# A transformer layer on one core: a batch's list of side work turned by eight groups, so that half of the left pieces and four Q and K pieces stand in the batch before

## The chip, the cores and the metric

The kernel runs on one core of a Trainium2 chip. The metric is device time in microseconds. Three runs of the kernel before gave 2230.23, 2231.86 and 2234.39 us: a median of 2231.86 us.

## The reference

The input is x of 8 batches, 1024 rows and 256 columns, in float32. The layer is an attention block with a residual and a layer norm, and a feed-forward block with the same around it.

```
Q, K, V = x Wq^T + bq, x Wk^T + bk, x Wv^T + bv        16 heads of 16 columns
scores  = Q K^T / 4 + lambda * mask                    mask[i, j]: two bells in |i - j|
x1      = layernorm(x + softmax(scores) V Wo^T + bo)
h       = x1 ternary(w_fc)^T + gate * (x1 v^T fast_b^T u^T)
out     = layernorm(x1 + max(h, 0)^2 ternary(w_proj)^T)
```

`ternary(w)` rounds each row of a weight matrix to -1, 0 or 1 times the mean size of the row. The hidden width is 1024.

## The kernel before, in words

**Groups.** The attention is worked through in groups. A batch has four sets of four heads; each set has two halves of 512 queries (a *step* is one set and one half); a step has 8 blocks of 128 keys. One group treats one block of keys for the four heads, so a step has 8 groups, a batch 64 and the kernel 512. We call a group's place in its batch +0 to +63.

In each group TensorE does, in this order: the scores `e` of the group (L714, four matmuls; where the block lies near the half's diagonal, four more from `prior` at L724 add the mask); the *pieces* of side work of this group; the scores `s` of the group twelve places later (L647, four matmuls), from which VectorE finds each query's maximum (L659); and the weighted sum `av` of the group before (L753, eight matmuls). ScalarE takes exponentials of `e` (L738). Scores share three PSUM buffers in turn. Each block of eight groups turns its finished maxima with a matmul (L675) at places +5, +13, +21 and so on; they go through DRAM (`rows`) into the stacks from which the scores are made (L691). Every sixteen groups `fill_stack` loads the stacks of a coming set, eight DMAs of 256 KB, at +0, +16, +32 and +48.

**Pieces.** All other work is cut into pieces for two small PSUM halves (`misc`), and each piece has a matmul part and an `empty` part that follows on ScalarE, GpSimd or VectorE:

- `transpose_x` (L540): turns a quarter of a half of x of the coming batch into `xT`; eight pieces. The two halves of x share one buffer, and the fourth piece asks for the second half.
- `queries_keys(b, c)` (L593): Q and K of eight heads, eight pieces, K and Q by turns for the first half of the rows and then for the second. Every second piece casts a full half into `two` (ScalarE, L612), subtracts on GpSimd (L613) and writes the result to DRAM (`parts_k`, `parts_q`). `two` has one buffer.
- `values` (L566): V, eight pieces.
- A *chunk* of 256 rows of the feed-forward: two projections P (L953), two turns T (L987), one low rank L (L1000), eight hidden H (L1027) and four output O (L1062). A batch has four chunks. `first_chunk` makes the first chunk's row load and the addition of its bias ride on other pieces.

Projections need the heads divided by their sums: `normalize` hangs steps on later groups. For the second half of the heads, these are a load of the sums at +1 of the next batch, an inversion at +3, loads at +4, and divisions of the two halves on GpSimd at +6 and +8 (L810).

Each P, Q/K and V piece has a cost number of 0.86, O 0.93, H 0.6, L 0.48, T 0.23 and `transpose_x` 0.22. A group has room for two halves of `misc`. While the rest of the list would fit into the rest of the batch at one piece a group, a group stops at a fill of over 0.75; otherwise it goes on.

**The list of a batch.** `jobs_of(b)` (L1372 to L1411) writes the batch's pieces in order. For batches 1 to 6 the list before is: the load of x; eight pieces of Q and K of the second half of the heads of this batch (`qk`), with the eight pieces left over from the list before (`over`) and the first four transposes of x of batch b + 1 among them; four V pieces; and the feed-forward of batch b - 1, with four transposes, the eight Q/K pieces of the first heads and four V pieces of batch b + 1 among it. The last eight pieces of it (four H, four O) are left over. Batch 0 has no feed-forward yet and prepares the ternary weights instead (L442, L475, L519), in which a chain of small VectorE instructions (L460 to L466) follows each row block. Batch 7 has no batch to prepare for. After group 511 the last batch's feed-forward runs alone.

Every engine executes its instructions in the order in which they are written; the waits are derived from the tiles.

Of the kernel before, what the change touches and what calls it, by code (L numbers as in the profile page):

```python
# [30 lines left out]
WIDE = LEFT + 8 * P  # L31

LEAD = 12

KEPT = 8


@with_exitstack
def tile_postln_layer(
# [21 lines left out]
    B, L, D = x.shape  # L61
    NH = D // HD
    NG = NH // HG
    NB = L // P
# [32 lines left out]
    def load_x(b, half, tag="x"):  # L97
        t = p1.tile([P, QB, D], F32, tag=tag, name=f"x_{b}_{half}")
        nc.sync.dma_start(t, x[b, ts(half, HALF), :].rearrange("(t p) d -> p t d", p=P))
        x_of[b, half] = t  # L100
# [261 lines left out]
    now, jobs = -LEAD, []  # L362
# [966 lines left out]
    def with_(f, piece):  # L1329
        return (piece[0], lambda: (f(), piece[1]())[1], *piece[2:])  # L1330
# [33 lines left out]
    over = []  # L1364

    def first_x(b, main):

        for f, n in zip(first_chunk[b][0], (-8, -2)):
            main[n] = with_(f, main[n])
        return main  # L1370

    def jobs_of(b):  # L1372


        qk = queries_keys(b, 1, misc)
        load, early_xv, ahead = [], [], []
        if b + 1 < B:
            load = [(0.0, lambda: load_x(b + 1, 0), 0)]
            xs, vs = transpose_x(b + 1, misc), values(b + 1, misc)
            early_xv, ahead = xs[:4] + vs[: NB // 2], xs[4:]  # L1380
            ahead = ahead + queries_keys(b + 1, 0, misc) + vs[NB // 2 :]
        if b + 1 < B:
            first_chunk[b] = chunk(b, 0, misc)
        if b == 0:
            main = [(0.3, prepare_v, 1)] + [u for i in range(2) for u in prepare_fc(i)]
            main += [u for i in range(D // P) for u in prepare_proj(i)]
            side = ahead[:12] + early_xv[4:] + ahead[12:]
            return load + qk + early_xv[:4], first_x(b, spread(main, side, 0.05, 0.9))
        old = [over[k : k + 2] for k in range(0, len(over), 2)] or [[]] * 4
        if ahead:  # L1390
            t, q, v = ahead[:4], ahead[4:12], early_xv[4:] + ahead[12:]

            lead = [t[0], t[1], q[0], t[2], q[1], t[3], q[2], q[3], v[4], q[4], q[5]]
            at_end = [[q[6], q[7]], [v[5], v[6]], [v[7]], []]
            main = v[:4] + feed_forward(b - 1, misc, lead, at_end)
            t = early_xv[:4]
        else:

            old_o = old[2] + old[3]
            t, old[2:], lead = [()] * 4, [[], []], [qk[6], qk[7], *old_o]  # L1400
            main, qk = feed_forward(b - 1, misc, lead), qk[:6]
            load = [(0.0, f, 0) for k in (2, 3) for f in (ends[k]["load"], ends[k]["bias"])]
            for f, n in zip((ends[0]["load"], ends[0]["bias"]), (-8, -2)):
                main[n] = with_(f, main[n])
        t = [list(u for u in (k,) if u) for k in t]
        jobs = load + [qk[0], *old[0], qk[1], *old[1], *qk[2:4]]

        jobs += [*old[2], *t[0], qk[4], *t[1], *old[3], *t[2], qk[5], *t[3], *qk[6:]]
        over[:] = main[-KEPT:] if b + 1 < B else []
        main = main[:-KEPT] if b + 1 < B else main  # L1410
        return jobs, first_x(b, main) if b + 1 < B else main  # L1411

    def ready(u):
# [47 lines left out]
        *e0["H"][4:],  # L1463
    ]
    rest, es = None, {}
    jobs = [u for part in jobs_of(0) for u in part]

    v_first, qk_first, jobs[:7] = values(0, misc), jobs[1:7], jobs[:1]
    early = [u for two in zip(v_first, qk_first) for u in two] + v_first[6:]
    for g in range(-LEAD, total + 1):  # L1470
# [5 lines left out]
        if 0 <= g < total and g % per_batch == 0:  # L1476
            if g:
                assert not jobs
                jobs = [u for part in jobs_of(g // per_batch) for u in part]
        if g == total - 7:  # L1480

            old, jobs = jobs, []
# [157 lines left out]
```

## Time and profile before

| What | us |
|---|---|
| median of three runs | 2231.86 |
| the profiled execution | 2231.73 |
| its span | 2229.9 |
| TensorE busy in the span | 2160.5 |
| VectorE busy | 1591.5 |
| ScalarE busy | 1442.7 |
| GpSimd busy | 902.7 |
| before group 0 | 59.7 |
| batch 0 | 254.2 |
| batch 1 | 265.8 |
| a middle batch | 263.7 |
| batch 7 | 260.7 |
| after the start of group 511 | 70.7 |

The rows of batches are times from the first `e` matmul of one batch to that of the next, by the timeline. The profile is one execution on the chip. PE is TensorE's matmul, PEld its weight load, DVE VectorE, ACT ScalarE, POOL GpSimd, SP the engine that issues most DMAs. A line of the timeline has the start in us, the length in us, the engine, the source line, the instruction, what it writes and reads, the shapes, a count, and in brackets the idle time of the engine before it and what ended that.

### The profile page before, as it was taken

To read this page: it belongs to the slowest core of one execution; us is meant where nothing else is said; L and a number is where in the kernel's file an instruction comes from. 1 tells how busy PE (TensorE), PEld (TensorE's weight loads), DVE (VectorE), ACT (ScalarE), POOL (GpSimd) and SP (SyncE) were. 2 spreads that over 40 slices of the span, in tenths; PEclk is the share of its full clock that TensorE was granted. 3 is DMA by queue.
4 is the path that set the end of the run, shared out by engine and by line. 5 is a ranking of instruction groups with operands and counts; after the bars stand their busy time and mean duration, and the time that the engine had idled before them with its cause. 6 is when DMAs were issued, how large, how long until landed. Compare 5 with 4: busy or idle time off the path is not lost.

```text
span 2229.9 us, 36851 instructions
## 1 busy us (share of the span) xinstructions
PE 2160.5 (97%) x13144; PEld 1258.9 (56%) x13144; DVE 1591.5 (71%) x2952; ACT 1442.7 (65%) x2155; POOL 902.7 (40%) x1024
## 2 busy tenths in 40 slices
PE   6999999999999999999999999999999999999997
PEld 3444445555555555556555555555655555555557
DVE  6777776777777776777777777677777777677736
ACT  2665566666666667666666667676666666666654
POOL 4133322445333453245533444335443345444444
PEclk8999999999999999999999999999999999999998
DMA  7433334123433224423333223421344321422010
GB/s 194 109 92 89 74 96 114 66 71 75 118 115 87 56 56 119 129 71 80 75 125 103 73 67 92 130 87 52 75 118 116 87 71 46 132 70 53 22 46 20
DMA packets 110572, 193.36 MB, mean 87 GB/s; under 512 B 21100, under 2 KB 50108, under 8 KB 110388
## 3 DMA queue, kind: packets, MB, share of 16 engines
q1 hardware_dynamic: 108972, 189.42, 30.8%
q8 instruction: 104, 1.70, 0.3%
q10 hardware_dynamic: 1416, 1.58, 0.2%
q14 instruction: 80, 0.66, 0.1%
HBM read 105.19 MB, written 85.69 MB: 86 GB/s over the span
## 4 chain that ended last, share of the span: by engine, by line
PE 82%; DVE 8%; POOL 1%; issue 1%; ACT 1%; DMA 1%; SPq 0%; POOLq 0%; DVEq 0%; ACTq 0%
PE e L714 22%; PE av L753 19%; PE s L647 15%; DVE junk L659 6%; PE e L724 5%; PE misc L1027 4%; PE misc L593 4%; PE misc L1062 4%; PE misc L953 2%; PE misc L566 2%; PE misc L1034 1%; ACT exp L738 1%; DVE st L911 1%; PE misc L987 1%; PE misc L540 0%
## 5 line engine op out<-in xcount | busy, mean ns | idle before, releaser
L659 DVE CUSTOM_DVE_ANT_0 junk<-s,wide 128x1024 f32<-128x1024 f32 x1024 | 1248.6, 1219 | 534.3 <-PE s L647 492.0
L738 ACT ACTIVATE exp<-e 128x1024 f32<-128x1024 f32 x1024 | 1027.6, 1025 | 622.4 <-PE e L724 376.3
L714 PE MATMUL e<-st_q,st_k 66*128 66x512 f32 (+1 forms) x2048 | 664.6, 425 | 0.6 <-ACT exp L738 0.3
L714 PEld LDWEIGHTS e<-st_q,st_k 66*128 66x128 f32 (+1 forms) x2048 | 324.1, 189 | 463.3 <-ACT exp L738 82.5
L753 PE MATMUL av<-exp,v 128*17 128x512 f32 x4096 | 540.8, 600 | 0.0
L647 PE MATMUL s<-st_k,st_q 64*128 64x512 f32 x2048 | 400.5, 447 | 43.7 <-DVE pm L659 26.7
L647 PEld LDWEIGHTS s<-st_k,st_q 64*128 64x128 f32 x2048 | 167.3, 185 | 179.5 <-DVE pm L659 66.7
L737 DVE TENSOR_TENSOR e<-e,wide 128x372 f32<-128x372 f32 (+2 forms) x376 | 190.8, 507 | 47.0 <-PE e L714 41.9
L1045 POOL TENSOR_TENSOR rl<-rl 128x512 f32<-128x512 f32 x112 | 116.6, 1041 | 250.8 <-ACT hi L1044 243.4
L724 PEld LDWEIGHTS e<-prior,ident_r 128*128 128x128 f32 x1056 | 159.7, 190 | 24.2
L753 PEld LDWEIGHTS av<-exp,v 128*17 128x17 f32 x4096 | 68.1, 95 | 185.6 <-issue 184.5
L724 PE MATMUL e<-prior,ident_r 128*128 128x244 f32 (+2 forms) x1056 | 157.7, 272 | 0.0
L1047 POOL TENSOR_TENSOR lo<-rl,hi 128x512 fp32r<-128x512 f32 x112 | 143.9, 1285 | 8.8
L576 POOL TENSOR_TENSOR v<-v,bv_row 128x256 f32<-128x256 f32 x64 | 43.8, 686 | 213.4 <-ACT v L575 213.4
L1082 POOL TENSOR_TENSOR r<-r,sp_row 128x256 f32<-128x256 f32 x56 | 41.2, 735 | 205.1 <-ACT r L1081 205.1
L1027 PE MATMUL misc<-xhi,wfT 128*128 128x256 f32 x448 | 116.0, 282 | 0.2 <-ACT fullq L608 0.2
L1027 PE MATMUL misc<-xlo,wfT 128*128 128x256 f32 x448 | 115.1, 280 | 0.0
L1062 PE MATMUL misc<-wpT,lo 128*128 128x256 f32 x448 | 111.7, 283 | 2.1 <-POOL lo L1047 2.1
L1062 PE MATMUL misc<-wpT,hi 128*128 128x256 f32 x448 | 113.8, 287 | 0.0
L613 POOL TENSOR_TENSOR twok<-fullk,twok 128x512 fp32r<-128x512 f32 x30 | 38.6, 1288 | 163.0 <-ACT twok L612 163.0
L1040 ACT ACTIVATE rl<-misc,s_fc 128x256 f32<-128x256 f32 x224 | 94.3, 475 | 0.2
L1062 PEld LDWEIGHTS misc<-wpT,lo 128*128 128x128 f32 x448 | 85.1, 190 | 6.3 <-POOL lo L1047 2.9
(241 smaller groups left out, 2353.8 us busy)
## 6 DMA issues: line engine op xcount, KB each, us to landing
st_k<-parts_k SPq DMA_DIRECT2D x128, 256.0 KB
st_q<-parts_q SPq DMA_DIRECT2D x124, 256.0 KB
parts_k<-twok SPq DMA_DIRECT2D x60, 512.0 KB
parts_q<-twoq SPq DMA_DIRECT2D x64, 256.0 KB
parts_q<-twoq SPq DMA_DIRECT2D x30, 512.0 KB
x<-in_L_attn_x_dram SPq DMA_DIRECT2D x16, 512.0 KB
raw_o<-avs SPq DMA_DIRECT2D x248, 32.0 KB
rec<-back SPq DMA_DIRECT2D x30, 256.0 KB
```

What stands on the lines that cost most here:

```text
L647: nc.tensor.matmul(pair[a][:, kh, :], stack["q", s, pr, a][rows, ts(blk, P)], stack["k", s, pr, a][rows, ts(kh, HALF)], start=True, stop=True,
L659: nc.vector.tensor_tensor_reduce(out=junk, in0=t.rearrange("p k n -> p (k n)"), in1=wide[:, LEFT - P * blk : LEFT - P * blk + L], scale=1. ...
L714: nc.tensor.matmul(t[:, a, :], stack["k", s, pr, a][rows, ts(blk, P)], stack["q", s, pr, a][rows, ts(h, HALF)], start=True, stop=not by_pe,)
L724: nc.tensor.matmul(t[:, a, lo - HALF * h : hi - HALF * h], ident_r, prior[:, n, lo - first : hi - first], start=False, stop=(n == 1),)
L737: nc.vector.tensor_add(part, part, add.to_broadcast([P, 2, hi - lo]))
L738: nc.scalar.activation(e, t.rearrange("p a n -> p (a n)"), AF.Exp)
L753: nc.tensor.matmul(av[32 * j : 32 * j + HD + 1, :], v_bufs[b % 2][:, blk, g * HG + j, : HD + 1], es[j // 2][:, ts(j % 2, HALF)], start=(n ...
L1027: nc.tensor.matmul(ph, wfT[:, dc, ts(hc, P)], st[k2][:, dc, :], start=(dc == 0 and k2 == "xhi"), stop=False,)
L1040: nc.scalar.activation(rl[:, ts(k, n)], ph, AF.Relu, scale=s_fc[:, hc : hc + 1])
L1045: nc.gpsimd.tensor_mul(rl, rl, rl)
L1047: sub(lo, rl, hi.bitcast(F32))
L1062: nc.tensor.matmul(py, st[k][:, hc, ts(i, P)], wpT[:, hc, :], start=(hc == 0 and k == "hi"), stop=(hc == NHC - 1 and k == "lo"),)
```

## The change

In batches 1 to 6 the list now begins where, eight groups earlier, it used to end. Of the second heads' Q and K of batch b + 1, the four pieces of the first rows (`r[0]` to `r[3]`) stand at the end of batch b, among the feed-forward's last pieces, and the other four (`kept_qk`) at the start of batch b + 1, with the four transposes of x that follow. Of the eight pieces left over, six are done in the same batch now (four H, two O), and two O pieces (`over`) are left. Batch 0 takes four Q/K pieces more, batch 1 six pieces of feed-forward more, and batch 7 has four Q/K and six feed-forward pieces fewer. x of batch b + 2 is asked for at the end of batch b in place of x of batch b + 1 at its start. No instruction is added or taken away on TensorE.

```
--- before.py
+++ after.py
@@ -31,8 +31,6 @@
 WIDE = LEFT + 8 * P
 
 LEAD = 12
-
-KEPT = 8
 
 
 @with_exitstack
@@ -1369,47 +1367,43 @@
             main[n] = with_(f, main[n])
         return main
 
+
+    kept_qk = []
+
     def jobs_of(b):
 
-
-        qk = queries_keys(b, 1, misc)
-        load, early_xv, ahead = [], [], []
+        load = []
+        if b + 2 < B:
+            load = [(0.0, lambda: load_x(b + 2, 0), 0)]
         if b + 1 < B:
-            load = [(0.0, lambda: load_x(b + 1, 0), 0)]
-            xs, vs = transpose_x(b + 1, misc), values(b + 1, misc)
-            early_xv, ahead = xs[:4] + vs[: NB // 2], xs[4:]
-            ahead = ahead + queries_keys(b + 1, 0, misc) + vs[NB // 2 :]
-        if b + 1 < B:
+            t, v = transpose_x(b + 1, misc), values(b + 1, misc)
+            q, r = (queries_keys(b + 1, c, misc) for c in range(2))
             first_chunk[b] = chunk(b, 0, misc)
         if b == 0:
             main = [(0.3, prepare_v, 1)] + [u for i in range(2) for u in prepare_fc(i)]
             main += [u for i in range(D // P) for u in prepare_proj(i)]
-            side = ahead[:12] + early_xv[4:] + ahead[12:]
-            return load + qk + early_xv[:4], first_x(b, spread(main, side, 0.05, 0.9))
-        old = [over[k : k + 2] for k in range(0, len(over), 2)] or [[]] * 4
-        if ahead:
-            t, q, v = ahead[:4], ahead[4:12], early_xv[4:] + ahead[12:]
-
-            lead = [t[0], t[1], q[0], t[2], q[1], t[3], q[2], q[3], v[4], q[4], q[5]]
+            side = [*t[4:], *q, *v, *r[:4]]
+            kept_qk[:] = r[4:]
+            first_load = (0.0, lambda: load_x(b + 1, 0), 0)
+            jobs = [first_load, *queries_keys(b, 1, misc), *t[:4]]
+            return [*jobs, *first_x(b, spread(main, side, 0.05, 0.9)), *load]
+        p = kept_qk[:]
+        if b + 1 < B:
+            kept_qk[:] = r[4:]
+
+            jobs = [t[0], p[0], t[1], *over, t[2], p[1], t[3], *p[2:], *v[:4]]
+
+            lead = [t[4], t[5], q[0], t[6], q[1], t[7], q[2], q[3], v[4], q[4], q[5]]
             at_end = [[q[6], q[7]], [v[5], v[6]], [v[7]], []]
-            main = v[:4] + feed_forward(b - 1, misc, lead, at_end)
-            t = early_xv[:4]
-        else:
-
-            old_o = old[2] + old[3]
-            t, old[2:], lead = [()] * 4, [[], []], [qk[6], qk[7], *old_o]
-            main, qk = feed_forward(b - 1, misc, lead), qk[:6]
-            load = [(0.0, f, 0) for k in (2, 3) for f in (ends[k]["load"], ends[k]["bias"])]
-            for f, n in zip((ends[0]["load"], ends[0]["bias"]), (-8, -2)):
-                main[n] = with_(f, main[n])
-        t = [list(u for u in (k,) if u) for k in t]
-        jobs = load + [qk[0], *old[0], qk[1], *old[1], *qk[2:4]]
-
-        jobs += [*old[2], *t[0], qk[4], *t[1], *old[3], *t[2], qk[5], *t[3], *qk[6:]]
-        over[:] = main[-KEPT:] if b + 1 < B else []
-        main = main[:-KEPT] if b + 1 < B else main
-        return jobs, first_x(b, main) if b + 1 < B else main
-
+            main = first_x(b, feed_forward(b - 1, misc, lead, at_end))
+            main, h, o = main[:-8], main[-8:-4], main[-4:]
+            over[:] = o[2:]
+            return [*jobs, *main, *load, r[0], *h[:2], r[1], *h[2:], r[2], r[3], *o[:2]]
+        main = feed_forward(b - 1, misc, [p[2], p[3]])
+        jobs = [(0.0, f, 0) for k in (2, 3) for f in (ends[k]["load"], ends[k]["bias"])]
+        for f, n in zip((ends[0]["load"], ends[0]["bias"]), (-8, -2)):
+            main[n] = with_(f, main[n])
+        return [*jobs, p[0], *over, p[1], *main]
 
 
     def ready(u):
@@ -1463,7 +1457,7 @@
         *e0["H"][4:],
     ]
     rest, es = None, {}
-    jobs = [u for part in jobs_of(0) for u in part]
+    jobs = jobs_of(0)
 
     v_first, qk_first, jobs[:7] = values(0, misc), jobs[1:7], jobs[:1]
     early = [u for two in zip(v_first, qk_first) for u in two] + v_first[6:]
@@ -1476,7 +1470,7 @@
         if 0 <= g < total and g % per_batch == 0:
             if g:
                 assert not jobs
-                jobs = [u for part in jobs_of(g // per_batch) for u in part]
+                jobs = jobs_of(g // per_batch)
         if g == total - 7:
 
             old, jobs = jobs, []
```

## The prediction

> **What bounds the kernel now.** I read the page first (span, busy shares, chain), then windows by batch, then the timeline group by group. A group is the work between the first `e` matmul (L714) of one pair of exponentials and that of the next; there are 512, 64 to a batch.
>
> ```profile
> span 2229.9 us, 36851 instructions
> PE 2160.5 (97%) x13144; PEld 1258.9 (56%) x13144; DVE 1591.5 (71%) x2952; ACT 1442.7 (65%) x2155; POOL 902.7 (40%) x1024
> ...
> PE 82%; DVE 8%; POOL 1%; issue 1%; ACT 1%; DMA 1%; SPq 0%; POOLq 0%; DVEq 0%; ACTq 0%
> ```
>
> TensorE is busy for 97% of the span and makes 82% of the chain. Total work doesn't change, so only idle TensorE time can move. Windows show where that idle time is: batch 0, batch 1, a middle batch, the first 15 groups of batch 7, the other 48, the end.
>
> ```profile
> 59.70:313.90 254.20, 237.75 (x1354) 120.85 (x1352) 195.04 (x372) 152.74 (x220) 69.96 (x77) 0.99 0.30 80
> 313.90:579.70 265.80, 261.17 (x1576) 148.82 (x1572) 190.17 (x347) 175.80 (x260) 100.36 (x112) 0.99 0.32 88
> 579.70:843.40 263.70, 262.09 (x1628) 153.26 (x1624) 190.39 (x351) 179.30 (x268) 108.62 (x122) 1.00 0.33 91
> 1898.50:1961.50 63.00, 60.94 (x366) 34.54 (x362) 43.88 (x79) 41.48 (x59) 26.27 (x29) 1.00 0.40 122
> 1961.50:2159.20 197.70, 193.01 (x1213) 114.78 (x1209) 126.47 (x249) 129.84 (x186) 97.50 (x113) 1.00 0.20 49
> 2159.20:2229.90 70.70, 55.48 (x380) 48.83 (x376) 42.06 (x90) 30.88 (x64) 28.20 (x40) 0.90 0.05 16
> ```
>
> (Start:end, length, then busy time of PE, PEld, DVE, ACT, POOL, granted clock, DMA share, GB/s.) Idle: 16.5 us in batch 0, 4.6 in batch 1, 1.6 in a middle batch, 2.1 in the 15 groups. A middle batch is full; batches 0, 1 and 7 decide.
>
> What does a piece cost? A group with none still takes 3.55 or 4.00 us:
>
> ```profile
> 302.41 1.20 PE L714 MATMUL e<-st_q,st_k 66*128 66x512 f32 x4
> ...
> 305.96 0.73 PE L714 MATMUL e<-st_q,st_k 66*128 66x512 f32 x2
> ...
> 309.96 0.73 PE L714 MATMUL e<-st_q,st_k 66*128 66x512 f32 x2
> ...
> 313.94 0.74 PE L714 MATMUL e<-st_q,st_k 66*128 66x512 f32 x2
> 315.42 1.03 PE L593 MATMUL misc<-xT,wkT 128*128 128x256 f32 x4
> ```
>
> These are the starts of groups 61 to 64; 61 (a turned maximum only) takes 3.55, 62 takes 4.00, 63 takes 3.98. Group 64 holds one Q/K piece and takes 4.08 (its 1.03 us of L593 adds 0.1); group 65, of the short kind, also with one, takes 3.65. By the same subtraction over a middle batch: V the same 0.1; output piece 0.17; two hidden pieces 0.4 (4.41, 3.95); two projections 0.95 (4.51); transpose and Q/K 0.3 (4.31, 3.87); transpose and two output pieces 1.35 (4.90). So some 0.75 us of fill is free in each group and the rest is paid in full: a piece moved into an empty group costs 0.1, and a group left empty gains only what its piece had cost above the floor.
>
> **The change, part by part.** The instruction order of both programs gives the pieces of each group.
>
> *Batch 7, groups 448 to 462* (from 463 on both are the same). Before, they hold 8 Q/K, 4 hidden, 4 output, 2 projection pieces and last 4.08, 3.96, 4.09, 3.94, 4.10, 3.75, 4.08, 4.06, 4.31, 4.52, 4.09, 5.56, 4.18, 4.25, 4.01: 63.0. After, 4 Q/K, 2 output and the 2 projections are left. Same kinds by rows: 4.08, 5.10 (two output pieces, as group 481), 4.09, 3.56, 4.01, 3.65, 3.98, 3.85, 3.91, 4.52, 4.09, 3.65, 4.01, 3.55, 4.01: 60.1. **-2.9.** Ends: -2.4 if group 456's unexplained 4.31 stays, -3.4 if the two output pieces cost what row 4.90 leaves for them.
>
> *Batch 0* takes four Q/K pieces (groups 48 to 54) into groups of the empty kind: 4 x 0.1 = +0.4. Its order shifts too, and there VectorE is held up: the chain that scales low rows (L460 to L466) runs at the start of eight groups.
>
> ```profile
> 161.93 1.28 POOL L613 TENSOR_TENSOR twoq<-fullq,twoq 128x512 fp32r<-128x512 f32 x1
> 162.14 1.11 DVE L461 TENSOR_SCALAR lowf<-lowf,inv,gate_c 128x16 f32<-128x16 f32 x1
> ...
> 165.21 1.22 PE L647 MATMUL s<-st_k,st_q 64*128 64x512 f32 x4 [1.96 <-DVE pm L659]
> ...
> 176.05 0.29 DVE L461 TENSOR_SCALAR lowf<-lowf,inv,gate_c 128x16 f32<-128x16 f32 x1
> ```
>
> L461 takes 0.29 to 0.44 in six of them and 1.11 and 1.29 beside GpSimd's L613 of a Q/K piece (groups 26 and 34: 6.59 and 5.43, that is 2.6 and 1.4 over the floor; the other six some 0.2 to 0.65 over). In the changed order of POOL three of the eight fall right beside such a subtraction (groups 20, 27, 32). Those three have transposes between the waits, as 34 and unlike 26, so I take 1.4 each: eight excesses of 0.65, 0.22, 0.58, 1.44, 0.75, 1.4, 0.65, 1.44 make 7.1 against 7.0 before. **Batch 0: +0.5.** Ends: all three at 2.6, +4; no collision, -2.5.
>
> [...]
>
> *Batch 1* loses a stall:
>
> ```profile
> 342.87 1.13 SPq L691 DMA_DIRECT2D st_q<-rows  x4
> 344.04 0.39 SPq L196 DMA_DIRECT2D parts_k<-twok  x1
> ...
> 348.60 0.62 ACT L612 CAST twoq<-fullq 128x512 fp32r<-128x512 f32 x1 [2.66 <-DMA parts_k<-twok]
> ```
>
> K's halves, ready at group 69, stood in SP's queue behind the maxima's round trip; Q's cast two groups later waits for that write, since `two` has one buffer; exponentials stand behind the cast on ScalarE. Groups 72 and 73 take 7.34 and 4.97 where rows of their kind have 4.00 and 3.65: 4.7. After, no K piece ends between groups 68 and 74, so nothing of that kind stands there. The batch gets six pieces more (4 hidden, 2 output); its list is then a middle batch's without the two output pieces at its second group (3.87 for 4.90): 263.7 - 1.1 = 262.6 against 265.8. **-3.1.** If a like stall stays: +1.6.
>
> *Batches 2 to 6.* Every piece stands eight groups sooner. Maxima turn every eight groups, so they keep their place; short and long groups repeat in sixteen, with the same count of each in a batch. The multiset is equal: **0.** Ends +-2 in all (one group in 320 showed 4.43 for 4.05). Moved past queues: next x halves are asked for at +55 and +3 in place of +0 and +11, rows for a later chunk eight groups sooner; each lands groups before its use, and their cover is that SP has no matmul behind it at those places. The projections move from +17 to +9, right after the heads are divided; the changed order makes them wait for the first half's division alone, which in batch 7 ended at 1926.45 where they started at 1935.96. That gate holds with 9 us to spare.
>
> Sum: -2.9 + 0.5 - 3.1 + 0 = -5.5. The profiled execution took 2231.73 (span 2229.9), the median is 2231.86, so no correction: **2226.4 us**, own range 2223.5 to 2229.5.
>
> **Rivals.** *A, a new wait in every batch, slower.* At +2 and +4 the K write and Q's cast now stand two groups apart (three before), behind eight stack loads. If the cast waits as at group 72, each of batches 1 to 6 pays 4.7: 28 - 5.5 gives 2254. It decides once write and landing take longer than two groups, 8.1 us. Against: at groups 65 and 67 of batch 1 the same spacing behind the same loads shows no wait (cast at 321.2, write at 323.2, Q's cast at 328.9 with 0.08 idle). A part of it, 1 to 2 us in six batches, would end at 2234 to 2239. The clock makes such a wait dear: after the stall of group 72 the granted clock was 0.62 from 350 to 358, and 0.59 from 165 to 169 after only 1.96 us of idle TensorE. [...]
>
> *B, the stall of batch 1 comes back elsewhere:* -5.5 + 4.7, 2231.0. For: batch 1's queue is the fullest at its start (three landings of 4 to 5 us in the chain). *C, collisions at group 26's price:* -5.5 + 3.5, 2229.9.
>
> **Chances.** Forecast 0.66, of which 0.58 are beyond 0.2% (4.5 us, about what a measurement of this kernel can tell from no change); B and C 0.21, of which 0.02; A and its parts 0.13. Faster 0.60, same 0.27, slower 0.13. The range from 2222 to 2233 takes in B, C and both ends of the forecast and leaves out A, and a little at each side.
>
> **What would show it.** Right: groups 451 to 462 mostly 3.55 and 4.0; no 7 us group in batch 1 and a granted clock of 1.00 there; batches 2 to 6 at 263.7; three L461 of over 1 us. Wrong: ScalarE's L612 with idle time behind a `parts_k` landing at +4 of the middle batches, projections at +9 behind POOL's L810, or batch 0 above 257.

## The result and the profile after

The changed kernel took 2245.92 us (median of four, 2244.91 to 2246.66) beside 2231.05 us for the kernel before (2227.33 to 2234.39): a ratio of 1.0062, 95% interval 1.0047 to 1.0078. It is slower by 14.9 us, where 5.5 us less were forecast. The profiled execution has a span of 2243.1 us for 2229.9. All lines of the changed kernel stand two lower from L31 on (L714 is now L712, L659 is L657, L647 is L645, L613 is L611, L461 is L459).

The page of the changed kernel: span, TensorE and VectorE, and the shares of the chain of waits.

```profile
span 2243.1 us, 36865 instructions
...
PE 2164.0 (96%) x13144; PEld 1258.6 (56%) x13144; DVE 1593.3 (71%) x2952; ACT 1443.6 (64%) x2155; POOL 903.1 (40%) x1024
...
PE 80%; DVE 9%; POOL 2%; issue 1%; DMA 1%; ACT 1%; SPq 0%; POOLq 0%; DVEq 0%; ACTq 0%
```

TensorE's busy time grew by 3.5 us with the same instructions, and the span by 13.2: some 10 us are idle time, which VectorE and GpSimd now end more often. The windows of the changed kernel show where (start:end, length, busy time of PE, PEld, DVE, ACT, POOL, granted clock, DMA share, GB/s): batch 0, batch 1, batch 3, the first 15 groups of batch 7, its other 48, the end.

```profile
60.10:321.00 260.90, 244.00 (x1371) 123.79 (x1369) 196.24 (x372) 155.86 (x226) 72.51 (x79) 0.99 0.32 88
321.00:586.60 265.60, 262.18 (x1613) 152.30 (x1609) 189.71 (x347) 179.24 (x267) 104.18 (x115) 0.99 0.32 88
...
852.07:1116.97 264.90, 262.32 (x1628) 153.48 (x1624) 190.78 (x351) 179.71 (x268) 111.39 (x125) 1.00 0.32 90
1911.83:1976.53 64.70, 56.74 (x314) 28.27 (x310) 44.37 (x81) 35.43 (x45) 20.76 (x26) 0.97 0.33 95
1976.53:2174.46 197.93, 193.01 (x1213) 114.89 (x1209) 126.14 (x247) 129.84 (x186) 94.09 (x109) 1.00 0.20 47
2174.50:2243.10 68.60, 53.44 (x380) 46.53 (x376) 42.16 (x90) 30.45 (x64) 28.20 (x40) 0.94 0.05 16
```

The 15 groups of batch 7 have 60.94 - 56.74 = 4.2 us less work on TensorE than before and yet last 64.7 us for 63.0. A middle batch has 2.6 us of idle TensorE for 1.6, at a clock of 1.00, and is 1.2 to 1.3 longer.

| Time from first `e` matmul to the next batch's, us | before | changed | difference | forecast |
|---|---|---|---|---|
| before group 0 | 59.7 | 60.1 | +0.4 | 0 |
| batch 0 | 254.3 | 260.9 | +6.6 | +0.5 |
| batch 1 | 265.8 | 265.6 | -0.2 | -3.1 |
| batches 2 to 6 together | 1318.8 | 1325.3 | +6.5 | 0 |
| batch 7 to group 511 | 260.7 | 262.6 | +1.9 | -2.9 |
| from group 511 on | 70.7 | 68.6 | -2.1 | 0 |
| sum | 2229.9 | 2243.1 | +13.2 | -5.5 |

Three places, then, need a cause: batch 7, batch 0 and the middle batches.

**Batch 7.** The timeline of the changed kernel (start, length, engine, line, instruction; in brackets the idle time before it and what ended that):

```profile
1922.09 2.80 POOL L1129 TENSOR_TENSOR x_last<-x_last,bo_row 128x256 f32<-128x256 f32 x4 [9.16 <-DMA x_last<-in_L_attn_x_dram]
...
1924.86 1.43 POOL L942 TENSOR_TENSOR x<-x,bo_row 128x256 f32<-128x256 f32 x2
...
1926.25 0.71 POOL L1080 TENSOR_TENSOR r<-r,sp_row 128x256 f32<-128x256 f32 x1
1927.05 0.72 POOL L1081 TENSOR_TENSOR r<-r,x 128x256 f32<-128x256 f32 x1
...
1927.80 0.43 DVE L909 BATCH_NORM_STATS2 st<-r 128x6 f32<-128x256 f32 x1 [2.72 <-POOL r L1081]
...
1929.62 0.73 PE L645 MATMUL s<-st_k,st_q 64*128 64x512 f32 x4 [3.68 <-DVE pm L657]
...
1930.28 1.86 PE L751 MATMUL av<-exp,v 128*17 128x512 f32 x8
```

GpSimd stood 9.16 us for the landing of `x_last` (two DMAs that SP issued behind the eight stack loads at the batch's start). Behind it, in GpSimd's order, stood the residual additions of the left-over output pieces, which the change had brought to +1. The layer norm's statistics (L909) waited for them on VectorE, the maxima behind the statistics, and TensorE's scores behind the maxima: 3.68 us idle, and `av` at 1.86 in place of 1.05 after it. The kernel before has the same wait of GpSimd, 6.9 us, but its output pieces stood at +11 and later:

```profile
1908.20 2.81 POOL L1131 TENSOR_TENSOR x_last<-x_last,bo_row 128x256 f32<-128x256 f32 x4 [6.90 <-DMA x_last<-in_L_attn_x_dram]
```

**Batch 0.** Three L611 fell beside the chain of the low rows, as forecast, at groups 20, 27 and 32. The first and, at 27, the next line of the chain:

```profile
138.45 1.29 POOL L611 TENSOR_TENSOR twok<-fullk,twok 128x512 fp32r<-128x512 f32 x1
138.50 1.27 DVE L459 TENSOR_SCALAR lowf<-lowf,inv,gate_c 128x16 f32<-128x16 f32 x1
...
140.45 1.22 DVE L657 CUSTOM_DVE_ANT_0 junk<-s,wide 128x1024 f32<-128x1024 f32 x1
...
141.73 1.29 PE L645 MATMUL s<-st_k,st_q 64*128 64x512 f32 x4 [0.82 <-DVE pm L657]
...
142.95 1.91 PE L751 MATMUL av<-exp,v 128*17 128x512 f32 x8
...
170.61 1.30 POOL L611 TENSOR_TENSOR twok<-fullk,twok 128x512 fp32r<-128x512 f32 x1 [0.49 <-ACT twok L610]
170.82 1.14 DVE L463 CAST ones_low<-lowf 128x32 fp32r<-128x32 f32 x1
```

Group 20 took 6.82 us for 4.51 before, 27 took 5.39 for 3.52, 29 (with no subtraction beside it) 5.34 for 4.22. In the second half of group 20 the matmuls ran at about half their rate (1.91 us for 1.05 elsewhere); the window says the same of the clock (0.52):

```profile
138.00:141.70 3.70, 2.17 (x15) 1.52 (x11) 3.49 (x11) 1.11 (x2) 1.74 (x2) 1.00 0.28 104
141.70:145.00 3.30, 3.27 (x13) 0.94 (x14) 2.48 (x4) 1.46 (x3) 0.00 (x0) 0.52 0.56 207
```

And at the batch's end, group 58 took 5.56 for 3.98:

```profile
293.95 1.29 POOL L808 TENSOR_TENSOR o<-o,rec 128x512 f32<-128x512 f32 x1
...
295.20 1.43 POOL L942 TENSOR_TENSOR x<-x,bo_row 128x256 f32<-128x256 f32 x2
...
296.61 1.14 POOL L392 TENSOR_SCALAR tern_proj<-proj,sc_proj 128x256 f32<-128x256 f32 x1
297.84 1.14 POOL L393 TENSOR_SCALAR proj<-proj,sc_proj 128x256 f32<-128x256 f32 x1
299.07 0.73 POOL L394 TENSOR_TENSOR proj<-proj,tern_proj 128x256 f32<-128x256 f32 x1
...
299.85 0.44 PE L517 MATMUL misc<-ident,proj 128*128 128x128 f32 x2 [1.91 <-POOL proj L394]
```

The ternary projection's three steps on GpSimd stand behind a division of heads and the addition of a bias. In the kernel before the projection's pieces stand at 56 to 59 in place of 55 to 58, and TensorE waits for none of them there.

**The middle batches.** The extra time is at fixed places. Sums of the four groups that a batch has at each place of sixteen, mean of batches 2 to 6; since pieces stand eight groups sooner, place p of the changed kernel is set beside p + 8 of before:

| pieces of before's place | before | the same pieces, changed | difference |
|---|---|---|---|
| 8 (now at 0) | 16.16 | 17.17 | +1.01 |
| 0 (now at 8) | 16.64 | 16.35 | -0.29 |
| 7 (now at 15) | 16.22 | 17.06 | +0.84 |
| 15 (now at 7) | 17.06 | 16.67 | -0.39 |
| the other twelve | 197.68 | 197.80 | +0.12 |

Groups at 7 and 8 are of another kind than those at 15 and 0. The timeline of the kernel before shows it in group 200 (place 8) and group 208 (place 0):

```profile
876.40 0.28 DVE L737 TENSOR_TENSOR e<-e,wide 128x116 f32<-128x116 f32 x1 [0.51 <-PE e L714]
877.73 0.28 DVE L737 TENSOR_TENSOR e<-e,wide 128x116 f32<-128x116 f32 x1
...
909.25 0.58 PE L724 MATMUL e<-prior,ident_r 128*128 128x186 f32 x4
...
910.42 0.55 DVE L737 TENSOR_TENSOR e<-e,wide 128x372 f32<-128x372 f32 x1
```

At 8 (and 7) the mask has 58 columns for each head, and VectorE adds them to both pairs; at 0 (and 15) TensorE adds the mask of one pair with L724. So at 8 TensorE has 0.58 us less of its own, and a group there takes 4.0 to 4.15 us with anything from one V piece to a transpose and a Q/K piece in it, while at 0 the same pieces are paid. Places 2 and 6 differ from 10 and 14 too (244 or 186 columns of mask), but the differences of these four sum to 0.0.

### The profile page after: what moved, and what is told of

The parts are those of the page before. It is cut to its first block, busy times and chain, and to the rows that moved or that the text cites. A ratio compares the mean times of both kernels' runs of the same rounds, so it can differ in the third digit from the quotient of the medians.

```text
span 2243.1 us, 36865 instructions
## 1 busy us (share of the span) xinstructions
PE 2164.0 (96%) x13144; PEld 1258.6 (56%) x13144; DVE 1593.3 (71%) x2952; ACT 1443.6 (64%) x2155; POOL 903.1 (40%) x1024
## 4 chain that ended last, share of the span: by engine, by line
PE 80%; DVE 9%; POOL 2%; issue 1%; DMA 1%; ACT 1%; SPq 0%; POOLq 0%; DVEq 0%; ACTq 0%
PE e L712 21%; PE av L751 19%; PE s L645 15%; DVE junk L657 6%; PE e L722 5%; PE misc L1025 4%; PE misc L1060 4%; PE misc L591 4%; PE misc L951 2%; PE misc L564 2%; PE misc L1032 1%; ACT exp L736 1%; DVE st L909 1%; PE misc L985 1%; DMA rows<-both 0%
## 5 line engine op out<-in xcount | busy, mean ns | idle before, releaser
L657 DVE CUSTOM_DVE_ANT_0 junk<-s,wide 128x1024 f32<-128x1024 f32 x1024 | 1249.1, 1220 | 544.1 <-PE s L645 501.7
L712 PE MATMUL e<-st_q,st_k 66*128 66x512 f32 (+1 forms) x2048 | 667.1, 426 | 1.7 <-DMA st_q<-rows 1.0
L712 PEld LDWEIGHTS e<-st_q,st_k 66*128 66x128 f32 (+1 forms) x2048 | 325.3, 189 | 466.7 <-ACT rl L1038 75.7
L645 PE MATMUL s<-st_k,st_q 64*128 64x512 f32 x2048 | 400.7, 447 | 47.9 <-DVE pm L657 29.7
L645 PEld LDWEIGHTS s<-st_k,st_q 64*128 64x128 f32 x2048 | 167.6, 185 | 184.7 <-DVE pm L657 66.6
L735 DVE TENSOR_TENSOR e<-e,wide 128x372 f32<-128x372 f32 (+2 forms) x376 | 190.7, 507 | 47.4 <-PE e L712 42.8
L611 POOL TENSOR_TENSOR twok<-fullk,twok 128x512 fp32r<-128x512 f32 x30 | 38.6, 1286 | 179.3 <-ACT twok L610 179.3
```

Source lines behind the costliest of these rows:

```text
L645: nc.tensor.matmul(pair[a][:, kh, :], stack["q", s, pr, a][rows, ts(blk, P)], stack["k", s, pr, a][rows, ts(kh, HALF)], start=True, stop=True,
L657: nc.vector.tensor_tensor_reduce(out=junk, in0=t.rearrange("p k n -> p (k n)"), in1=wide[:, LEFT - P * blk : LEFT - P * blk + L], scale=1. ...
L712: nc.tensor.matmul(t[:, a, :], stack["k", s, pr, a][rows, ts(blk, P)], stack["q", s, pr, a][rows, ts(h, HALF)], start=True, stop=not by_pe,)
L735: nc.vector.tensor_add(part, part, add.to_broadcast([P, 2, hi - lo]))
```

## The experiments

### The bias of x_last later

```diff
-        jobs = [(0.0, f, 0) for k in (2, 3) for f in (ends[k]["load"], ends[k]["bias"])]
+        jobs = [(0.0, ends[k]["load"], 0) for k in (2, 3)]
+        late = [(0.0, ends[k]["bias"], 0) for k in (2, 3)]
...
-        return [*jobs, p[0], *over, p[1], *main]
+        return [*jobs, p[0], *over, p[1], *late, *main]
```

> The changed kernel, but in batch 7 the two additions of the bias to the last rows stand behind the two left-over output pieces and the second Q/K piece. Theory (a wait in GpSimd's order): in the changed kernel's trace GpSimd waits 9.2 us for the last rows' landing, the output pieces' sums stand behind it, VectorE waits 2.7 us for them and TensorE 3.7 us for VectorE; without it groups 451 and 452 take 3.6 and 4.0 in place of 7.34 and 4.73, and the time falls by 4.5 us, 2245.9 to 2241.4. Rival (empty groups: TensorE idles too long in the emptied list, and the clock falls): 451 stays at 7.3 and the time at 2245.9.

Measured: 2240.98 us (2239.77 to 2245.25), ratio 1.0046, interval 1.0033 to 1.0058, beside 2231.25 for the kernel before. Groups 451 and 452 took 3.73 and 3.95; the first 15 groups of batch 7 took 60.3 and the batch 258.3. GpSimd's timeline in this kernel:

```profile
1918.44 0.73 POOL L1080 TENSOR_TENSOR r<-r,sp_row 128x256 f32<-128x256 f32 x1 [5.24 <-ACT r L1079]
1919.25 0.73 POOL L1081 TENSOR_TENSOR r<-r,x 128x256 f32<-128x256 f32 x1
...
1926.46 2.82 POOL L1129 TENSOR_TENSOR x_last<-x_last,bo_row 128x256 f32<-128x256 f32 x4
```

The residual additions now wait for their own piece alone, and the bias waits for nothing. The cause in batch 7 is shown, and it was worth 4.4 us there (262.63 to 258.25).

### Batch 0's list in its old order

```diff
-            side = [*t[4:], *q, *v, *r[:4]]
+            side = [*t[4:], *q, *v]
...
-            return [*jobs, *first_x(b, spread(main, side, 0.05, 0.9)), *load]
+            return [*jobs, *first_x(b, spread(main, side, 0.05, 0.9)), *load, *r[:4]]
...
-                among = len(jobs)
+                among = len(jobs) - 5
...
-                behind = len(jobs) > among * (1 - (g + 1) / (per_batch - 3))
+                behind = g > 57 or len(jobs) - 5 > among * (1 - (g + 1) / (per_batch - 3))
```

The four Q/K pieces stand alone in groups 60 to 63, and the groups before them are those of the kernel before.

> The changed kernel, but batch 0 keeps the order it had before up to group 59, and its four further Q/K pieces stand alone in groups 60 to 63. Theory (where the preparation's VectorE and GpSimd steps meet, set by the order): batch 0 goes from 260.9 back to 254.7 (254.3 and four times 0.1), the time falls by 6 us, to 2240. Rival (the four pieces cost TensorE time wherever they stand in batch 0): four times 0.9 stays, batch 0 is 258 or more, the time falls by 3 us at most.

Measured: 2245.53 us (2241.94 to 2248.67), ratio 1.0062, interval 1.0049 to 1.0075. Batch 0 took 253.4 us, 7.5 less than in the changed kernel: its loss is the order of its list, and the four pieces themselves cost 0.5 together (groups 60 to 63). But the time did not fall by the 6 us expected: batch 1 took 268.8, since group 68 now took 8.78, and batches 2 to 6 took 2.1 us more than in the changed kernel. The timeline around group 68:

```profile
316.27 0.36 SPq L194 DMA_DIRECT2D parts_q<-twoq  x1
...
318.13 0.61 SPq L296 DMA_DIRECT2D st_k<-parts_k  x1
...
328.37 0.38 SPq L194 DMA_DIRECT2D parts_k<-twok  x1
...
334.80 0.62 ACT L610 CAST twoq<-fullq 128x512 fp32r<-128x512 f32 x1 [4.42 <-DMA parts_k<-twok]
...
336.63 1.29 PE L645 MATMUL s<-st_k,st_q 64*128 64x512 f32 x4 [3.21 <-DVE pm L657]
```

That is the stall of rival A: K's half was cast at 322.28, in group 65, and its write went out at 328.37, behind the eight stack loads and the heads' stores; Q's cast in group 68 found `two` still in use. K's cast stands where it does in the changed kernel. What differs is the pair before, which ends in group 63 and not in 54: its Q write (316.27) is ahead of the stack loads, which start 3.6 us after the batch's start, where in the changed kernel they start 3.4 us before it.

### H sooner, Q/K later at +56 to +59

```diff
+    def alone(u):
+        return (*u[:2], 2, *u[3:])
...
-            return [*jobs, *main, *load, r[0], *h[:2], r[1], *h[2:], r[2], r[3], *o[:2]]
+            return [*jobs, *main, *load, *h[:2], alone(r[0]), *h[2:], alone(r[1]), r[2], r[3], *o[:2]]
```

> The changed kernel, but at the end of batches 1 to 6 hidden pieces stand at places +56 and +58 and single Q/K pieces at +57 and +59, the other way round than in it. Theory (place 8 of 16 takes 4.0 to 4.1 us whatever of up to 1.2 us of pieces it holds, so it should hold the large one): 4.05, 3.65, 4.41, 3.65 in place of 4.16, 3.96, 4.08, 3.95, which is -0.39 in a batch and -2.3 us in all, 2243.6. Rival (all places of a kind alike, and the middle batches' 1.2 us come from waits): the four sum to 16.1 as before, 2245.9.

Measured: 2249.42 us (2245.74 to 2251.64), ratio 1.0075, interval 1.0061 to 1.0090. At +56 (place 8) two hidden pieces took 4.15 us, what one Q/K piece had taken there (4.14): the flat price of place 8 is confirmed. But the four groups together went only from 16.12 to 16.03 (+57 3.96 to 3.85, +58 4.08 to 4.39, +59 3.94 to 3.64), so the expected gain of the exchange was put too high. The time did not fall; in the profiled execution batch 0 took 262.5 and the end 75.2, neither of which this edit touches. That execution is one of the slowest of the six; why the median is 3.5 us above the changed kernel's stays open.

### Batch 1 begins with a fourth Q/K piece

```diff
-            side = [*t[4:], *q, *v, *r[:4]]
-            kept_qk[:] = r[4:]
+            side = [*t[4:], *q, *v, *r[:3]]
+            kept_qk[:] = r[3:]
...
-            jobs = [t[0], p[0], t[1], *over, t[2], p[1], t[3], *p[2:], *v[:4]]
+            jobs = [p.pop(0)] if b == 1 else []
+            jobs += [t[0], p[0], t[1], *over, t[2], p[1], t[3], *p[2:], *v[:4]]
```

> The changed kernel, but the last of the four Q/K pieces that batch 0 took stands at the start of batch 1, so that group 72 holds a V piece and is not empty; batch 0 has other meetings of small VectorE chains and GpSimd subtractions (by the order after groups 19, 27 and 31). Theory (the empty group 72 lets TensorE idle, the clock falls, and 72 and 73 take 4.77 and 5.41): they take 4.1 and 4.5, batch 1 falls by 1.6, less 0.1 for the piece; batch 0 with three meetings stays near 259 (254.7 and one meeting more than before, up to 2.6, and what follows it); together 2242 to 2245. Rival (72 and 73 wait for the division of the heads on GpSimd): 73 stays over 5, batch 1 at 265.6.

Measured: 2244.93 us (2240.48 to 2249.16), ratio 1.0058, interval 1.0044 to 1.0073. Groups 72 and 73 took 4.15 and 4.51 for 4.77 and 5.41 in the profiled execution of the changed kernel. But they took 4.09 and 4.52 under the late bias too, with group 72 as empty as in the changed kernel. So the filling is not what mends it: the 1.5 us belong to that one execution. The result doesn't tell the two theories apart.

### The kernel before, batch 1 pushed back

```diff
-        jobs += [*old[2], *t[0], qk[4], *t[1], *old[3], *t[2], qk[5], *t[3], *qk[6:]]
+        if b == 1:
+            jobs += [k for u in t for k in u] + [*main[:3], qk[4], qk[5], main[3], *qk[6:]]
+            main = main[4:]
+        else:
+            jobs += [*old[2], *t[0], qk[4], *t[1], *old[3], *t[2], qk[5], *t[3], *qk[6:]]
```

> The kernel before, with the order of batch 1's list alone changed: the four transposes come right behind the first four pieces of Q and K of the second heads, and the last four of these come after three pieces of V, so that no K half ends between groups 68 and 74 and Q's cast no longer waits behind the maxima for K's write. Theory (the stall at groups 72 and 73 is the order's, and it is all that batch 1 had to give): groups 72 and 73 about 4.1 and 3.7 for 7.34 and 4.97, batch 1 about 261 for 265.8, other batches as before; time about 2226.5, ratio about 0.998. Rival (the changed kernel's batch 1 became shorter because of what it does with its pieces, or the wait comes back where the last four pieces now stand, groups 74 to 78): batch 1 stays at 264 to 266 and the time at 2230 to 2232.

Measured: 2239.93 us (2236.17 to 2241.57), ratio 1.0039, interval 1.0025 to 1.0052, beside 2229.93. Groups 72 and 73 fell to 4.10 and 3.65 as the theory had it; but group 116 took 11.62 for 4.41, and batch 1 took 271.8. The timeline there:

```profile
517.87 0.40 SPq L1076 DMA_DIRECT2D out_dram<-r  x1
...
523.81 0.59 SPq L938 DMA_DIRECT2D x<-in_L_attn_x_dram  x1
...
531.83 1.41 POOL L944 TENSOR_TENSOR x<-x,bo_row 128x256 f32<-128x256 f32 x2 [10.79 <-DMA x<-in_L_attn_x_dram]
...
538.11 1.29 PE L647 MATMUL s<-st_k,st_q 64*128 64x512 f32 x4 [5.73 <-DVE pm L659]
```

The list ran about one group late here, so the output's write, which heads SP's queue ahead of the stack loads and the load of rows, went out 5.4 us later (512.45 in the kernel before); the rows landed late, GpSimd stood at their bias, and maxima and scores stood behind. It is the wait of batch 7 in another place: a bias on GpSimd behind a load that is late. Group 116 lost 7.2 us by it. Groups 74 to 115, with the list pushed back, took another 3.8 us more than before, and in this execution groups 503 to 505, which the edit does not touch, took 3.5.

### The kernel before, batch 1 exchanged within ten groups

```diff
+        if b == 1:
+            (t0,), (t1,), (t2,), (t3,) = t
+            jobs = [*jobs[:-1], t0, qk[3], t1, qk[4], qk[5], t2, t3, main[0], qk[6], qk[7], *main[1:4]]
+            main = main[4:]
```

> The kernel before, with the order of batch 1's list changed in groups 67 to 76 alone: the first two transposes one group sooner, the last two together, one V piece at 71, and the last two Q pieces at 72 and 73 in place of 70 and 71, behind the landing of K's write; from group 77 on every group holds the same pieces as in the kernel before. Theory (the 4.7 us at groups 72 and 73 come from Q's cast standing three groups too soon for K's write, and what went wrong at group 116 when the whole list was pushed back by a group was the push): groups 72 and 73 about 4.1 and 3.7 for 7.34 and 4.97, groups 77 to 127 as before, batch 1 about 261.3 for 265.8, time about 2226.5, ratio 0.998. Rival (the wait moves along: Q's cast at 73 still waits, or V's first piece waits for the transposes): one group between 67 and 75 takes 5 to 8 us, batch 1 265 or more, time 2230 or more.

Measured: 2228.85 us (2226.05 to 2231.94) beside 2230.80 (2227.95 to 2235.94), ratio 0.9990, interval 0.9980 to 0.9999. Batch 1 took 261.0; groups 72 and 73 took 4.09 and 3.65, and groups 77 to 127 take what they take in the kernel before within 0.06. The casts and writes of this kernel:

```profile
340.30 0.62 ACT L612 CAST twok<-fullk 128x512 fp32r<-128x512 f32 x1
...
345.68 0.39 SPq L196 DMA_DIRECT2D parts_k<-twok  x1
...
355.89 0.62 ACT L612 CAST twoq<-fullq 128x512 fp32r<-128x512 f32 x1
```

K's write goes out 5.4 us behind its cast (6.9 in the kernel before), and Q's cast now comes ten microseconds behind the write and waits for nothing. So spacing alone ends the stall, and this version is the only one here that is below both kernels. Its batch 1 gained 4.8 us and the medians differ by 2.0; the interval reaches to -4.5 us, and in the profiled execution the start and group 1 took 3.0 us more than in that of the kernel before. Two profiled executions with the old list of batch 1 paid the stall (groups 72 and 73: 7.34 and 4.97 in the kernel before, 7.35 and 5.37 in its version with both halves alike); whether every execution does wasn't measured.

### Late bias, and batch 0 old with three Q/K pieces at its end

The edits of the first two experiments, with `*r[:3]` and 4 for `*r[:4]` and 5, `kept_qk[:] = r[3:]`, and the fourth piece at the start of batch 1 as in the fourth.

> The changed kernel with the late x_last bias and batch 0's list in its old order; of the four Q and K pieces three stand alone in groups 60 to 62, the fourth at the start of batch 1, so that the casts of the four pairs around the batch's end are three, two and two groups apart in place of two each. Theory (batch 0's loss is the order of its list, and the stall at group 68 comes from pairs two groups apart behind the stack loads): batch 0 about 253.5 for 259.4, groups 68 and 69 about 4.1 and 3.7, batch 1 about 264, batch 7 258.3; time about 2235. What is left over the kernel before is then the steady batches (+1.2 each, some 6) and next to nothing else. Rival (any four pairs that follow each other across the batch's end stall once, wherever they stand): one group between 66 and 74 takes 7 to 9 us, batch 1 about 268.5, and the time stays at 2239 to 2241.

Measured: 2238.52 us (2233.02 to 2240.24), ratio 1.0033, interval 1.0021 to 1.0045. Group 68 took 4.33, batch 1 took 263.9 and batch 7 258.5: no pair waits when the casts stand in groups 61, 64, 66 and 68, with the three groups across the stack loads, as the theory had it. Batch 0 took 256.2; the 2.7 us over the expected 253.5 are in group 1 (5.51 for 3.93, long before the edit) and in group 26 (6.61; it was 5.25 under the old order alone). The time is between the two theories. In the profiled execution, the slowest of the six, start and end took 4.0 us more than in that of the kernel before, batches 2 to 6 took 6.7 and batch 0 1.9 more, and batches 1 and 7 took 4.1 less. The middle batches are thus the largest part of what remains.

### Late bias, and the output pieces away from +1

```diff
-            jobs = [t[0], p[0], t[1], *over, t[2], p[1], t[3], *p[2:], *v[:4]]
+            jobs = [t[0], p[0], t[1], p[1], t[2], p[2], t[3], p[3], *v[:4], *over]
```

> The changed kernel with the late x_last bias, and in batches 1 to 6 the two left-over output pieces at +8 and +9 in place of +1: +1 holds a transpose and a Q/K piece (as +3, 3.87, where it took 4.9), +8 an output piece in place of a V piece, and the second output piece pushes a projection, a turned piece and a V piece by a group each. Theory (a group of the kind of +8, whose mask columns VectorE adds, takes 4.0 to 4.15 whatever up to 1.2 us of pieces it holds; all other groups pay by the piece over their floor): +8 stays at 4.1, +1 falls by 1.0, +9 to +16 gain 0.5 to 0.8 together; a steady batch about 264.6 for 264.9, the time 1 to 2 us under 2241, about 2239. Rival (the pieces are paid wherever they stand): a steady batch 264.9 to 265.2, the time about 2241.

Measured: 2243.22 us (2237.41 to 2245.68), ratio 1.0055, interval 1.0038 to 1.0072. A middle batch took 265.0. Group +1 fell from 4.90 to 3.86 and +8 stayed at 4.10, but +9 to +16 grew by 1.1 (+11 3.86 to 4.25, +14 3.95 to 4.32, +15 4.09 to 4.31, +9 by 0.1). The rival is right: what leaves one group is paid in others. Place 8 gave nothing, for the V piece that it lost had been free there too. That the median is 2.2 us above that of the late bias alone does not come from the middle batches (265.0 for 265.2) and stays open.

### Late bias, and batch 0's subtractions on VectorE

```diff
-                nc.gpsimd.tensor_sub(two[:, 1, :], full, two[:, 0, :].bitcast(F32))
+                sub = nc.vector.tensor_sub if 0 < now < 64 else nc.gpsimd.tensor_sub
+                sub(two[:, 1, :], full, two[:, 0, :].bitcast(F32))
```

> The changed kernel with the late x_last bias, and in batch 0 the subtractions of the Q and K pieces (seven of 128x512) go to VectorE in place of GpSimd, so that no GpSimd subtraction stands beside the small VectorE chain of the low rows. Theory (the collisions at groups 20, 27 and 32 and the clock that they cost make most of batch 0's 6.6 us): L459 takes 0.3 to 0.45 in all eight groups, groups 20, 27 and 32 fall by about 1.4 each or more, batch 0 about 255 to 256 for 259.4, time about 2237. [...]

Measured: 2237.52 us (2236.96 to 2238.43), ratio 1.0035, interval 1.0023 to 1.0047. The two lines of the chain in this kernel, with minimum, median and maximum in nanoseconds:

```profile
L459 DVE TENSOR_SCALAR lowf<-lowf,inv,gate_c x8: 293/294/296, 110.2 to 194.6; 128x16 f32<-128x16 f32 x8
...
L463 DVE CAST ones_low<-lowf x16: 173/179/183, 110.5 to 195.2; 128x32 fp32r<-128x32 f32 x16
```

No collision is left, and batch 0 still took 259.6. Groups 20 and 32 took 5.15 and 5.12, but 27 took 6.61 and 29 5.75. A subtraction on VectorE takes 0.69 to 0.88 us and stands in the same place, in front of the chain and the maxima. So in this execution it cost as much to have the subtraction's work before a maximum, in a group without slack, as to have the collision there. That this is what costs is read from these rows; group 29, which holds no subtraction in either kernel, is late in both. And the median did fall by 3.5 us beside the late bias, as the theory had it, though the two profiled executions show none of it in batch 0 (1.6 of it is the start). Something else did change: group 58 took 4.07 for 5.55, for GpSimd, rid of seven subtractions of 1.3 us, came to the projection's three steps sooner. That part of batch 0's loss is GpSimd's order.

### Both halves of queries alike

To test the kinds of places by themselves, the second half of queries takes its key blocks in another order, so that places 8 to 15 are of the same kinds as 0 to 7. Pieces and groups are unchanged. The edit was made in the kernel before and in the changed kernel with the late bias.

```diff
-    order = {0: (0, 5, 1, 6, 2, 7, 3, 4), 1: (3, 0, 4, 1, 5, 2, 6, 7)}
+    order = {0: (0, 5, 1, 6, 2, 7, 3, 4), 1: (4, 0, 5, 1, 6, 2, 7, 3)}
```

> The kernel before, in which the second half of queries goes through its eight key blocks in the order 4, 0, 5, 1, 6, 2, 7, 3 in place of 3, 0, 4, 1, 5, 2, 6, 7, so that both halves treat the blocks of one kind at the same place: places 8 to 15 of sixteen are then of the same kinds as 0 to 7 (mask by TensorE at 0 and 8, the 58 columns by VectorE at 7 and 15). Pieces and their groups are the same. Theory (a list turned by eight groups costs more because places 7 and 8 are of another kind than 15 and 0, and nothing else): places 8 and 15 now take what the same pieces take in the changed kernel at 0 and 7, 17.17 for 16.16 and 16.67 for 17.06 in the four of a batch, so a steady batch goes from 263.8 to about 264.4 and the time up by some 3 to 5. Rival (the loss is in what is asked for and when, in the queues): a steady batch stays at 263.8.

> The changed kernel with the late x_last bias and the same new order of key blocks in the second half of queries. Theory (kinds of places): places 8 and 15 take what the same pieces take in the kernel before at 0 and 7, 16.64 for 16.35 and 16.22 for 17.06, so a steady batch goes from 265.1 to about 264.5: the difference between the two lists, 1.3 in each steady batch, falls to 0.1 or less when all eight-group halves are alike. Time some 3 under the late bias alone, about 2238. Rival (the queues, or something else that the turn brings): the difference between the two lists stays at 1.0 to 1.3 in a steady batch.

Measured, beside 2231.48 us for the kernel before: 2234.79 (2230.83 to 2240.24), ratio 1.0016, interval 1.0004 to 1.0028; and 2237.60 (2235.41 to 2239.48), ratio 1.0026, interval 1.0016 to 1.0037.

| mean of batches 2 to 6 | old list | turned list | difference |
|---|---|---|---|
| halves as they were | 263.76 | 265.19 | +1.43 |
| halves alike | 264.40 | 264.43 | +0.03 |
| pieces of before's place 8 (8 and 0), halves alike | 17.17 | 17.19 | +0.02 |
| pieces of before's place 15 (15 and 7), halves alike | 16.50 | 16.60 | +0.10 |

(265.19 is the late-bias kernel; its batch 2 took 266.0.) The loss of the middle batches is gone when the halves are alike, with every queue and every moved load as in the turned list. It is shown to be the kinds of places. The turned list is still 2.8 us slower in the median with the halves alike; in the two profiled executions batch 0 is 9.2 us longer, and batches 1 and 7 are 6.1 shorter.

## Why the prediction was wrong

**The step that failed most is "Batches 2 to 6: ... The multiset is equal: 0."** It counted short and long groups, which indeed repeat, and overlooked a third kind: at 7 and 8 VectorE adds the whole mask, at 15 and 0 TensorE adds half of it. A turn by eight exchanges them, and since the price of a piece depends on the slack of its group, the sum changes: +6.5 for 0. With the halves alike the difference between the lists is +0.03 a batch, which leaves next to nothing for another cause. The profile showed the third kind: groups 199 and 200 have no L724, 207 and 208 have it.

**Batch 7, -2.9.** The sum of the pieces' prices was right: with the late bias the 15 groups took 60.3 for a forecast 60.1. In part that is luck, for the two output pieces took 0.4 us less than forecast (4.70 for 5.10) and groups 451, 454, 455 and 456 0.2 to 0.3 more each. What was missing is a wait: the text says what each group holds, not what stands ahead of its pieces on GpSimd. The changed order puts the residual additions of `over` behind the bias of `x_last`, and the profile of before showed GpSimd idle 6.9 us in front of that bias. Measured +1.9 for the batch.

**Batch 0, +0.5.** Three collisions came, in the groups named. The terms that were mis-sized: 1.4 for each of the three measured 1.4 to 2.7 (group 20), 1.9 to 3.2 (27) and 1.3 to 2.9 (32 with 33) over the executions; of the chains without a collision, in the order of the sum, 0.75 for group 25 measured 0.8, but 0.65 for group 29 measured 0.9 to 2.1. And GpSimd's order at the end (groups 56 and 58, +2.0) was not looked at. The four pieces cost about what was said. Rival C's price of 2.6 lies within or near these ranges, but C had only that in it. The +6.6 is the difference of two executions: with the old order batch 0 took 252.8 to 255.8 us in four, with the changed order 259.4 to 262.5 in five.

**Batch 1, -3.1.** The stall of 4.7 went, and no cast waited in its place. The batch took 264.0 in the executions whose group 72 was undisturbed, for a forecast 262.6: it had been worked out from a middle batch of the kernel before (263.7), where a middle batch of the turned list, 265.05, less the 1.0 for the two output pieces, gives 264.0. It is the same mistake a second time. In the profiled execution of the changed kernel a further 1.5 was lost at 72 and 73:

```profile
355.85 0.82 PE L645 MATMUL s<-st_k,st_q 64*128 64x512 f32 x4 [1.15 <-issue]
356.60 1.72 PE L751 MATMUL av<-exp,v 128*17 128x512 f32 x8
358.26 2.08 PE L712 MATMUL e<-st_q,st_k 66*128 66x512 f32 x4
```

**The rivals.** A did not come in the changed kernel. Its spacing, K's cast and Q's two groups apart behind the stack loads, held:

```profile
328.75 0.62 ACT L610 CAST twok<-fullk 128x512 fp32r<-128x512 f32 x1
...
330.76 0.38 SPq L194 DMA_DIRECT2D parts_k<-twok  x1
...
336.88 0.62 ACT L610 CAST twoq<-fullq 128x512 fp32r<-128x512 f32 x1
```

The reasons against A were thus right; how near the edge it is was seen in the run with batch 0's old order, where the pair before, moved next to the batch's end, sent the stack loads out later. (The weaker form of A was mis-added: 1 to 2 us in six batches on 2226.4 make 2232.4 to 2238.4 and not 2234 to 2239.) The projections at +9 waited for nothing (4.52, as before). None of the rivals named the mechanism that decided, and the 0.13 for slower rested on A alone.

The turned list as it could be at best, late bias and old batch 0, is still slower by 0.2 to 0.45%. The gain that the change has to give, the stall of batch 1 and an emptier batch 7, is there (-1.9 and -2.2 us); the price of the turn in the middle batches is larger.

## What to carry to other kernels

Before a schedule is called the same, list what the host groups themselves contain at the old and the new places, mask work and the engine that does it included: work that was free in one group is paid in the next (the pieces of place 8, 16.16 us in a batch's four groups, took 17.17 at place 0). For each moved piece, read what stands ahead of its follow-up on the engine that does it: the kernel before had GpSimd's wait for `x_last` too (6.90 us), and it became a loss of 4.4 us when output pieces were put behind it. And one stall is best cured where it stands: ten groups reordered with all else in place gained 2.0 us in the median, barely clear of the noise, where turning the whole list lost 14.9, and where pushing the batch's list back cured the same stall and made a longer one at a later load.

## What the runs showed that had not been expected

The same rows do not take the same time in each execution. Group 27 of the changed batch 0, with the same instructions in the same order, took 5.39 us in two executions and 6.74 in two others; group 29 took 4.43 to 5.66. The difference is in the matmuls behind the idle time, which run at 0.73 and 1.05 us (`s`, `av`) or at 1.22 to 1.29 and 1.91. In group 20 a granted clock of 0.52 (`av` at 1.91) followed idle times of 0.74 and 0.82 us, in groups 72 and 73 a granted clock of 0.62 from 355.80 to 360.10 (`av` at 1.72) followed 1.15. In group 29 of the changed kernel 1.49 us of idle time were followed by `av` at 1.91, and VectorE's next addition of a mask (L735) began 2.76 us behind the start of the maximum before it; under the late bias it began 1.26 us behind. What decides at which of the two speeds a group goes on, no run here shows.

A VectorE cast of 32 columns (L463) took 1.14 us beside GpSimd's subtraction and 0.18 without it, as L459 did (1.27 and 0.29). The three of the changed kernel that began beside a subtraction, in groups 20, 27 and 32, ended 0.03 to 0.05 us behind its end (139.77 and 139.74, 171.96 and 171.91, 195.34 and 195.31); with the subtractions on VectorE no L459 took over 0.30 us and no L463 over 0.18. Why they end together no run here shows. In that execution, without any collision, batch 0 took 259.6 us beside 259.4 under the late bias, so to remove the collisions was not enough.

The part before group 0 took 59.7 to 62.5 us and the part from group 511 on 68.6 to 75.2 over the profiled executions, in kernels that are alike there. What sets this was not tried; it is the size of the effects looked for here, and it is why the readings above are made group by group.
